# A mixture-of-experts layer: each expert's weights and row numbers are read together with the last quarter of its rows

## The chip, the core and the metric

The kernel runs on one core of a Trainium2 chip. The metric is the device time of one execution in microseconds. Three runs of the kernel before gave 1192.09, 1194.07 and 1198.56 us; the median is 1194.07 us. One further execution was taken by the hardware profiler: it took 1184.45 us, and all durations and instants below are from it, counted from the start of its span.

The core has five engines with an instruction stream each: TensorE (PE; its weight loads are PEld), VectorE (DVE), ScalarE (ACT), GpSimd (POOL) and SyncE (SP). SP only issues transfers here, and GpSimd issues transfers with row numbers taken from a tile (indirect DMA). All transfers run on 16 DMA engines.

## The reference

The input `x` is 16 x 128 x 512 in float32. Two blocks follow each other, each with a residual:

```
x = x + xattn(layernorm(x), ctx)          # 8 heads over 128 channels, rotary positions
x = x + ffn(layernorm(x))                 # a mixture of 32 experts, over 2048 rows of 512

def ffn(rows):                            # the second block, cut to what matters
    logits = rows @ gate_w.T              # 2048 x 32
    sel_w, sel_e = top_k(logits, 8)
    w = softmax(sel_w)                    # 8 weights for each row, scattered to 2048 x 32
    g, u = rows @ w_gate_proj[e].T, rows @ w_up_proj[e].T      # 192 wide, each expert e
    return sum over e of (silu(g) * u * w[:, e]) @ w_down_proj[e].T
```

The kernel computes only the chosen pairs of row and expert.

## The kernel before

**The attention stage** (to about 620 us) normalizes, attends and projects 16 blocks of 128 rows. For each row it also computes the 8 experts, the weights and a slot in each chosen expert's list. An expert's list has `CAP` = 576 slots in `xslot`, a DRAM tensor of 32 x 576 rows of `ROW` = 560 floats. A row there is 512 normalized values, then the row's 32 weights (from column `WCOL` = 512), then its row number in the output (column `NCOL` = 544), then padding; 2240 bytes in all. GpSimd writes such rows to their slots by indirect DMA (`put`, L519 to L530).

**The expert stage** goes through 32 places `i`. The first `GIVEN` = 4 places are fixed experts (31 to 28), of which slots 0 to 255 (`EARLY`) are computed inside the attention stage (`early_read`, `early_turn`, `early_up`, `early_down`, `early_add`), with small tiles of their own. The other 28 experts are sorted by their number of rows, and place `i` computes `SIZES[i]` slots: 576 down to 516 at places 4 to 21, 512 to 492 at places 22 to 31. Which expert stands at a place is known only when the kernel runs, so from place 4 on its weights are picked by a mask, `whose` (L800). Each expert passes through these steps:

- `fetch(i)` (L1008), on SP: `read_rows` (L816) reads the slots' rows into `xg`, four transfers, one for each quarter of 128 columns. Quarter `a` goes to partitions 32a to 32a+31; slot 32b + j lands on partition 32a + j, at block b. `read_notes` (L839) then reads weights and row number of each slot, the notes, into a tile of another shape: slot 128m + p on partition p, column m. It takes one transfer for the first 512 slots (L847), one for the rest if there is any (L849), and at odd places a third for the row numbers of the rest (L851). Then come the expert's own matrices, `wgu` (L113) and `wd` (L114).
- `prepare(i)` (L1027), on VectorE: `turn_rows` (L828) transposes 32 x 32 blocks, so that `xt` holds the rows' columns on partitions (L833). `use_notes` (L854) makes the row numbers whole numbers (`to`, L859 and L861) and multiplies the 32 weights by the mask and sums them (L869, L875), so that `weight` has one number for each slot. At the four given places the expert is known and the weight is taken straight from the notes tile.
- `up` (L878): three chains of four products on TensorE for each half of the slots (L892), into PSUM tiles of `ps_u` (four of them); silu on ScalarE (L901, L904), and the product with the other half's result on VectorE (L902, L910).
- `down` (L918): products with `wd` (L927, L931), then the multiplication by `weight`, one tile of 128 slots on ScalarE (L972), the next on VectorE (L970). `settle_rest` (L977) does the slots past 512 of two places at once: the odd place's rest lies on partitions 64 on, so that its weights must lie there too (`REST` = 64), while its row numbers lie from partition 0.
- `add` (L943), on GpSimd: one indirect DMA for each tile of 128 slots adds it to the output's rows (L946). The adds of one expert may run beside each other; those of the next wait until they have landed, since a row has several experts.

**What sets the order.** Instructions stand on each engine's stream as the code issues them (`manual_schedule`). At place `i` the code issues `fetch(i + 2)`, then the first half of `up(i)`, then `prepare(i + 1)` (on VectorE it thus stands between the two halves of `up`), the second half, and `down` of place `i - 1`. `xg` has two buffers: the rows for place `i + 2` are read once those of place `i` have been used. `to`, `notes` and `weight` have four: `use_notes(i)` waits until the adds of place `i - 4` have read `to`. `yb`, the weighted outputs, has three.

Of the kernel before, what the change touches and what calls it, by code (L numbers as in the profile page):

```python
# [10 lines left out]
F32 = mybir.dt.float32  # L11
I32 = mybir.dt.int32
AF = mybir.ActivationFunctionType
ALU = mybir.AluOpType
AX = mybir.AxisListType
PSUM = bass.MemoryType.PSUM

P = 128
B, C, T = 16, 128, 512
# [4 lines left out]
E, I, TOPK = 32, 192, 8  # L24
# [4 lines left out]
CAP = 576  # L29
HALF = CAP // 2  # L30
NB = CAP // 32
FULL, REST = divmod(CAP, P)
NM = FULL + 1
# [3 lines left out]
GIVEN = 4  # L37
# [6 lines left out]
EARLY, CUT = 256, 13  # L44
# [4 lines left out]
WCOL, NCOL = T, T + E  # L49
# [10 lines left out]
def kernel(  # L60
# [16 lines left out]
    nc = tc.nc  # L77
# [32 lines left out]
    def load_expert(e, name):  # L110

        wgu_sb, wd_sb = new_weights(name)
        nc.sync.dma_start(wgu_sb, wgu[e])  # L113
        nc.sync.dma_start(wd_sb, wd[e])  # L114
        return wgu_sb, wd_sb
# [5 lines left out]
    with ExitStack() as actx:  # L121
# [528 lines left out]
        ready = []  # L650
# [162 lines left out]
        nc.vector.tensor_reduce(most, beyond, AX.XY, ALU.max)  # L813
        nc.vector.tensor_copy(over, most)

    def read_rows(rows, n, name, pieces=1, begin=0):  # L816

        xg = xp.tile([P, CAP // 32, P], F32, tag="xg", name=f"xg{name}")
        step = (n - begin) // 32 // pieces
        for b0 in range(begin // 32, n // 32, step):  # L820
            for a in range(4):
                nc.sync.dma_start(
                    xg[32 * a : 32 * (a + 1), b0 : b0 + step, :],
                    rows[32 * b0 : 32 * (b0 + step), a * P : (a + 1) * P].rearrange("(b j) q -> j b q", j=32),
                )
        return xg

    def turn_rows(xg, n, name, pieces=1, begin=0):  # L828

        xt = xp.tile([P, NK, CAP], F32, tag="xt", name=f"xt{name}")  # L830
        step = (n - begin) // 32 // pieces
        for b0 in range(begin // 32, n // 32, step):
            nc.vector.transpose(  # L833
                xt[:, :, 32 * b0 : 32 * (b0 + step)].rearrange("p c (b j) -> p b c j", j=32),
                xg[:, b0 : b0 + step, :].rearrange("p b (c i) -> p b c i", i=32),
            )
        return xt

    def read_notes(i, rows, n):  # L839

        notes = xp.tile([P, NM, E + 1], F32, tag="notes", name=f"notes_{i}", bufs=4)
        more = max(n - FULL * P, 0)
        half = slice(i % 2 * REST, i % 2 * REST + more)
        full = rows[0 : FULL * P, WCOL : NCOL + 1].rearrange("(m p) w -> p m w", p=P)
        nc.sync.dma_start(notes[:, 0:FULL, :], full)  # L847
        if more:
            nc.sync.dma_start(notes[half, FULL, :], rows[FULL * P : n, WCOL : NCOL + 1])  # L849
            if i % 2:  # L850
                nc.sync.dma_start(notes[0:more, FULL, E : E + 1], rows[FULL * P : n, NCOL : NCOL + 1])  # L851
        return notes

    def use_notes(i, notes, n):  # L854

        to = xp.tile([P, NM], I32, tag="to", name=f"to_{i}", bufs=4)
        more = max(n - FULL * P, 0)
        half = slice(i % 2 * REST, i % 2 * REST + more)
        nc.vector.tensor_copy(to[:, 0:FULL], notes[:, 0:FULL, E])  # L859
        if more:  # L860
            nc.vector.tensor_copy(to[0:more, FULL : FULL + 1], notes[0:more, FULL, E : E + 1])  # L861
        if i < GIVEN:
            return notes[:, :, E - 1 - i], to

        own = xp.tile([P, NM, E], F32, tag="own", name=f"own_{i}")
        weight = xp.tile([P, NM], F32, tag="weight", name=f"weight_{i}", bufs=4)
        for part, m0, m1 in ((slice(0, P), 0, FULL), (half, FULL, NM))[: 1 + (more > 0)]:
            k = part.stop - part.start
            nc.vector.tensor_tensor(  # L869
                own[part, m0:m1, :],  # L870
                notes[part, m0:m1, 0:E],
                whose[part, i - GIVEN, :].unsqueeze(1).to_broadcast([k, m1 - m0, E]),
                ALU.mult,
            )
            nc.vector.tensor_reduce(weight[part, m0:m1], own[part, m0:m1, :], AX.X, ALU.add)  # L875
        return weight, to

    def up(w, xt, n, name, parts=None, h=None, between=None):  # L878
# [129 lines left out]
    def fetch(i):  # L1008


        if i < GIVEN:
            e = E - 1 - i
        else:
            e = nc.values_load(
                numbers[0:1, i - GIVEN : i - GIVEN + 1],
                engines=[mybir.EngineType.SP],
                min_val=0,
                max_val=E - 1,
                skip_runtime_bounds_check_because="the lowest five bits",
            )  # L1020
        n = SIZES[i]
        rows = xslot[e * CAP : (e + 1) * CAP, :] if i < GIVEN else xslot[bass.ds(e * CAP, CAP), :]
        xg = read_rows(rows[:, 0:T], -(-n // 32) * 32, f"_{i}", 1 if i else 2, EARLY * (i < GIVEN))
        notes = read_notes(i, rows, n)
        return ready[i] if i < GIVEN else load_expert(e, i), xg, notes

    def prepare(i, w, xg, notes):  # L1027
        n = SIZES[i]
        xt = turn_rows(xg, -(-n // 32) * 32, f"_{i}", 1 if i else 2, EARLY * (i < GIVEN))
        return w, xt, use_notes(i, notes, n)  # L1030


    with tc.manual_schedule(engines=set(mybir.ALL_ENGINES) - {mybir.EngineType.Pool}):
# [210 lines left out]
```

## Time and profile before

| what | value |
|---|---|
| median of three runs | 1194.07 us |
| profiled execution, its own time | 1184.45 us |
| its span, first to last instruction | 1182.7 us |
| mean granted TensorE clock | 0.987 |
| transfers of SP (q1): packets, MB, share of 16 engines | 137640, 135.17, 43.4% |
| transfers of GpSimd (q0): packets, MB, share of 16 engines | 32608, 76.85, 27.9% |
| packets under 512 bytes, of all | 38308 of 177829 |
| VectorE: turned rows, L833 | 33 in 74.2 us |
| VectorE: row numbers, L859 | 32, median 129 ns |

The page of a profile gives busy time and number of instructions of each engine, the groups of instructions that cost most (line, engine, operation, output<-inputs, shapes, number; then busy time and mean, then the idle time of the engine ahead of them and what ended it) and the queues of transfers. In a timeline a line has the start, the length, engine, code line, operation, tiles and number, and in brackets the idle time before it and what ended that. Such a releaser is inferred: where an instruction waits for several things, the name is that of the one that came last by the profile. A share of the DMA engines over 1 is possible, as packets of several queues overlap.

### The profile page before, as it was taken

How to read it: one execution, taken by the hardware profiler on the slowest of the kernel's cores; microseconds unless marked ns; L12 is line 12 of the kernel's file. 1: busy time of each engine (PE TensorE's matmuls, PEld its weight loads, DVE VectorE, ACT ScalarE, POOL GpSimd, SP SyncE). 2: the span in 40 equal slices, each digit the busy share in tenths (PEclk: the TensorE clock that was granted, in tenths of full speed). 3: DMA queues.
4: the chain of work that ended last, by engine and by line, in shares of the span. 5: the costliest groups of instructions: out<-in, count | busy, mean ns of one | idle time of the engine just before them, and what ended most of it. 6: DMA issues, size and time to landing. Idle time of an engine off the chain costs nothing. (4 is left out here: it accounts for less than half of the span.)

```text
span 1182.7 us, 17253 instructions
## 1 busy us (share of the span) xinstructions
PE 1136.4 (96%) x5868; PEld 568.8 (48%) x5868; DVE 703.6 (59%) x1432; ACT 442.9 (37%) x833; POOL 609.0 (51%) x629
## 2 busy tenths in 40 slices
PE   7999999999999999999989999999999999999990
PEld 3333333333333333333365566676666667777670
DVE  5777878888888887887554453444444344433430
ACT  1266656566556655556541111112112121211120
POOL 3324443467877888665446333453443445434444
PEclk9999999999999999999999999999999999999995
DMA  5878888857566767453459899999999999999955
GB/s 181 289 279 309 315 306 315 312 200 240 184 201 215 245 229 259 147 186 145 139 173 251 158 246 233 205 230 207 211 208 189 212 207 228 229 232 215 172 75 70
DMA packets 177829, 255.51 MB, mean 216 GB/s; under 512 B 38308, under 2 KB 108580, under 8 KB 177736
## 3 DMA queue, kind: packets, MB, share of 16 engines
q1 hardware_dynamic: 137640, 135.17, 43.4%
q0 software_dynamic: 32608, 76.85, 27.9%
q10 hardware_dynamic: 7488, 42.34, 9.2%
q8 instruction: 48, 0.79, 0.3%
q14 instruction: 45, 0.37, 0.1%
HBM read 114.63 MB, written 131.01 MB: 208 GB/s over the span
## 5 line engine op out<-in xcount | busy, mean ns | idle before, releaser
L345 DVE TENSOR_REDUCE maxes_sb<-s 128x1 f32<-128x512 f32 x512 | 329.3, 685 | 97.1 <-PE s L340 78.9
L946 POOL DMA_INDIRECT out_dram<-yb,to x142 | 219.5, 1546 | 287.9 <-DMA out_dram<-yb,to 110.9
L347 ACT ACTIVATE p<-s 128x512 f32<-128x512 f32 x512 | 278.2, 594 | 217.6 <-PE s L340 209.1
L892 PE MATMUL psu<-xt,wgu 128*128 128x252 f32 (+19 forms) x1416 | 328.4, 392 | 3.9 <-DVE xt L833 2.6
L332 PE MATMUL s<-k,q 32*128 32x512 f32 x1024 | 313.8, 640 | 1.4 <-DVE maxes_sb L345 1.1
L892 PEld LDWEIGHTS psu<-xt,wgu 128*128 128x128 f32 x1416 | 267.4, 191 | 76.5 <-ACT yb L972 14.3
L340 PE MATMUL s<-qa,k 32*128 32x512 f32 x1024 | 292.9, 641 | 2.1 <-ACT p L347 2.1
L332 PEld LDWEIGHTS s<-k,q 32*128 32x128 f32 x1024 | 93.9, 183 | 155.9 <-DVE maxes_sb L345 121.8
L521 POOL DMA_INDIRECT xslot<-row,slot x128 | 130.2, 1017 | 36.4 <-issue 33.5
L369 PE MATMUL av<-p,vt_sb 128*32 128x512 f32 x1024 | 137.0, 608 | 0.0
L927 PE MATMUL psy<-wd,h 128*128 128x512 f32 x240 | 108.5, 592 | 0.0
L281 POOL TENSOR_TENSOR straight<-straight,rope_sb 128x512 f32<-128x512 f32 x31 | 39.4, 1272 | 124.0 <-DMA other<-straight 108.3
L970 DVE TENSOR_SCALAR yb<-psy,weight 128x512 f32<-128x512 f32 (+5 forms) x56 | 42.1, 751 | 90.3 <-PE psy L931 87.4
L904 ACT ACTIVATE s<-psu 64x252 f32<-64x252 f32 (+19 forms) x59 | 22.8, 386 | 191.9 <-PE psu L892 178.5
L910 DVE TENSOR_TENSOR h<-psu,s 64x128 f32<-64x128 f32 (+16 forms) x166 | 43.0, 259 | 75.8 <-ACT s L904 74.1
L340 PEld LDWEIGHTS s<-qa,k 32*128 32x128 f32 x1024 | 78.6, 183 | 10.7 <-ACT p L347 10.5
L972 ACT ACTIVATE yb<-psy,weight 128x512 f32<-128x512 f32 x56 | 38.5, 687 | 118.8 <-PE psy L931 114.7
L902 DVE TENSOR_TENSOR h<-psu,s 128x252 f32<-128x252 f32 (+19 forms) x59 | 25.7, 436 | 88.2 <-PE psu L892 87.0
L833 DVE STREAM_TRANSPOSE xt<-xg 128x2176 f32<-128x2176 f32 (+4 forms) x33 | 74.2, 2251 | 1.1
L369 PEld LDWEIGHTS av<-p,vt_sb 128*32 128x32 f32 x1024 | 20.4, 108 | 97.2 <-issue 78.8
L927 PEld LDWEIGHTS psy<-wd,h 128*128 128x128 f32 x240 | 45.3, 189 | 44.8 <-issue 41.2
L931 PE MATMUL psy<-wd,h 64*128 64x512 f32 x240 | 60.4, 618 | 0.0
(139 smaller groups left out, 915.6 us busy)
## 6 DMA issues: line engine op xcount, KB each, us to landing
xslot<-empty_sb ACTq DMA_DIRECT2D x48, 840.0 KB
wgu<-in_wgu_dram SPq DMA_DIRECT2D x28, 768.0 KB
wd<-in_wd_dram SPq DMA_DIRECT2D x28, 512.0 KB
xg<-xslot SPq DMA_DIRECT2D x48, 272.0 KB
xg<-xslot SPq DMA_DIRECT2D x40, 256.0 KB
other<-straight SPq DMA_DIRECT2D x64, 128.0 KB
spread<-straight SPq DMA_DIRECT2D x64, 128.0 KB
k<-spread SPq DMA_DIRECT2D x32, 256.0 KB
```

The costliest lines, as they stand in the source:

```text
L332: nc.tensor.matmul(p1, q[rows, tt * P : (tt + 1) * P], k[rows, :], start=True, stop=True)
L340: nc.tensor.matmul(p2, k[rows, sc * P : (sc + 1) * P], qa[rows, :], start=True, stop=True)
L345: nc.vector.tensor_reduce(to, p1, AX.X, ALU.max)
L347: nc.scalar.activation(pr, p2, AF.Exp, scale=HD**-0.5)
L369: nc.tensor.matmul(av[j * SLOT : (j + 1) * SLOT, :], vt[:, at : at + SLOT], pairs.pop((u, sc, j)), start=(sc == 0), stop=(sc == NT - 1),)
L521: op = nc.gpsimd.indirect_dma_start(out=xslot[0 : (E - k) * CAP, :], out_offset=bass.IndirectOffsetOnAxis(ap=st["slot", b][:, k : k + 1], ...
L833: nc.vector.transpose(xt[:, :, 32 * b0 : 32 * (b0 + step)].rearrange("p c (b j) -> p b c j", j=32), xg[:, b0 : b0 + step, :].rearrange("p ...
L892: nc.tensor.matmul(p[:, 0:half], wgu_sb[:, kk, ch * P : (ch + 1) * P], xt[:, kk, cols], start=(kk == 0), stop=(kk == NK - 1),)
L910: nc.vector.tensor_tensor(h2[to : to + IR, lo:hi], ps[2][IR:P, at], s2[IR:P, at], ALU.mult)
L927: nc.tensor.matmul(y, h1[:, rows], wd_sb[:, 0, :], start=True, stop=False)
L931: nc.tensor.matmul(y, h2[to : to + IR, rows], wd_sb[to : to + IR, 1, :], start=False, stop=True,)
L946: op = nc.gpsimd.indirect_dma_start(out=out, out_offset=bass.IndirectOffsetOnAxis(ap=to[0:k, m : m + 1], axis=0), in_=yb[0:k, m, :], in_of ...
```

## The change

The notes are no longer read by themselves. The tile `xg` gets 33 more columns in each block (161 floats, 644 bytes, where there were 128 floats, 512 bytes), and the transfer of the last quarter reads 161 columns instead of 128, so that weights and row numbers land behind the last 128 values, on partitions 96 to 127: slot 32b + j on partition 96 + j, at block b. The transposes read 128 of the 161 columns.

`use_notes` now works from there. From place 4 on it multiplies by the mask and sums on these 32 partitions, for all blocks at once (512 to 576 elements for each partition). Then it copies row numbers and weights into the old layout: block b belongs to partitions 32(b mod 4) on of column b // 4, so for each of the four groups of 32 partitions one copy to `to` and one to `weight` takes all full columns, and each block past slot 512 takes two more, its weights 64 partitions higher at odd places. The given places copy their weights too, for the blocks from slot 256 on. In the instruction streams VectorE has 376 instructions in `use_notes` where it had 146, and SP 65 transfers fewer. The early part of the four given experts keeps its notes as they were.

```diff
@@ -813,15 +813,17 @@
         nc.vector.tensor_reduce(most, beyond, AX.XY, ALU.max)
         nc.vector.tensor_copy(over, most)
 
-    def read_rows(rows, n, name, pieces=1, begin=0):
-
-        xg = xp.tile([P, CAP // 32, P], F32, tag="xg", name=f"xg{name}")
+    def read_rows(rows, n, name, pieces=1, begin=0, more=0):
+
+
+        xg = xp.tile([P, CAP // 32, P + E + 1], F32, tag="xg", name=f"xg{name}")
         step = (n - begin) // 32 // pieces
         for b0 in range(begin // 32, n // 32, step):
             for a in range(4):
+                k = P + more * (a == 3)
                 nc.sync.dma_start(
-                    xg[32 * a : 32 * (a + 1), b0 : b0 + step, :],
-                    rows[32 * b0 : 32 * (b0 + step), a * P : (a + 1) * P].rearrange("(b j) q -> j b q", j=32),
+                    xg[32 * a : 32 * (a + 1), b0 : b0 + step, 0:k],
+                    rows[32 * b0 : 32 * (b0 + step), a * P : a * P + k].rearrange("(b j) q -> j b q", j=32),
                 )
         return xg
 
@@ -832,47 +834,41 @@
         for b0 in range(begin // 32, n // 32, step):
             nc.vector.transpose(
                 xt[:, :, 32 * b0 : 32 * (b0 + step)].rearrange("p c (b j) -> p b c j", j=32),
-                xg[:, b0 : b0 + step, :].rearrange("p b (c i) -> p b c i", i=32),
+                xg[:, b0 : b0 + step, 0:P].rearrange("p b (c i) -> p b c i", i=32),
             )
         return xt
 
-    def read_notes(i, rows, n):
-
-
-
-        notes = xp.tile([P, NM, E + 1], F32, tag="notes", name=f"notes_{i}", bufs=4)
-        more = max(n - FULL * P, 0)
-        half = slice(i % 2 * REST, i % 2 * REST + more)
-        full = rows[0 : FULL * P, WCOL : NCOL + 1].rearrange("(m p) w -> p m w", p=P)
-        nc.sync.dma_start(notes[:, 0:FULL, :], full)
-        if more:
-            nc.sync.dma_start(notes[half, FULL, :], rows[FULL * P : n, WCOL : NCOL + 1])
-            if i % 2:
-                nc.sync.dma_start(notes[0:more, FULL, E : E + 1], rows[FULL * P : n, NCOL : NCOL + 1])
-        return notes
-
-    def use_notes(i, notes, n):
-
-        to = xp.tile([P, NM], I32, tag="to", name=f"to_{i}", bufs=4)
-        more = max(n - FULL * P, 0)
-        half = slice(i % 2 * REST, i % 2 * REST + more)
-        nc.vector.tensor_copy(to[:, 0:FULL], notes[:, 0:FULL, E])
-        if more:
-            nc.vector.tensor_copy(to[0:more, FULL : FULL + 1], notes[0:more, FULL, E : E + 1])
+    def use_notes(i, xg, n):
+
+
+
+        first, last = (EARLY if i < GIVEN else 0) // 32, -(-n // 32)
         if i < GIVEN:
-            return notes[:, :, E - 1 - i], to
-
-        own = xp.tile([P, NM, E], F32, tag="own", name=f"own_{i}")
-        weight = xp.tile([P, NM], F32, tag="weight", name=f"weight_{i}", bufs=4)
-        for part, m0, m1 in ((slice(0, P), 0, FULL), (half, FULL, NM))[: 1 + (more > 0)]:
-            k = part.stop - part.start
+            weights = xg[3 * 32 : P, :, P + E - 1 - i]
+        else:
+
+            own = xp.tile([P, CAP // 32, E], F32, tag="own", name=f"own_{i}", bufs=1)[3 * 32 : P, 0:last, :]
             nc.vector.tensor_tensor(
-                own[part, m0:m1, :],
-                notes[part, m0:m1, 0:E],
-                whose[part, i - GIVEN, :].unsqueeze(1).to_broadcast([k, m1 - m0, E]),
+                own,
+                xg[3 * 32 : P, 0:last, P : P + E],
+                whose[3 * 32 : P, i - GIVEN, :].unsqueeze(1).to_broadcast([32, last, E]),
                 ALU.mult,
             )
-            nc.vector.tensor_reduce(weight[part, m0:m1], own[part, m0:m1, :], AX.X, ALU.add)
+            weights = xp.tile([P, CAP // 32], F32, tag="sum", name=f"sum_{i}", bufs=1)[3 * 32 : P, :]
+            nc.vector.tensor_reduce(weights[:, 0:last], own, AX.X, ALU.add)
+        to = xp.tile([P, NM], I32, tag="to", name=f"to_{i}", bufs=4)
+        weight = xp.tile([P, NM], F32, tag="weight", name=f"weight_{i}", bufs=4)
+        full = min(last, 4 * FULL)
+        for q in range(4):
+            rows, m0 = slice(32 * q, 32 * (q + 1)), first // 4
+            m1 = m0 + len(range(first + q, full, 4))
+            nc.vector.tensor_copy(to[rows, m0:m1], xg[3 * 32 : P, first + q : full : 4, P + E])
+            nc.vector.tensor_copy(weight[rows, m0:m1], weights[:, first + q : full : 4])
+        for b in range(full, last):
+            q = b % 4
+            nc.vector.tensor_copy(to[32 * q : 32 * (q + 1), FULL : FULL + 1], xg[3 * 32 : P, b : b + 1, P + E])
+            q += i % 2 * (REST // 32)
+            nc.vector.tensor_copy(weight[32 * q : 32 * (q + 1), FULL : FULL + 1], weights[:, b : b + 1])
         return weight, to
 
     def up(w, xt, n, name, parts=None, h=None, between=None):
@@ -1020,14 +1016,13 @@
             )
         n = SIZES[i]
         rows = xslot[e * CAP : (e + 1) * CAP, :] if i < GIVEN else xslot[bass.ds(e * CAP, CAP), :]
-        xg = read_rows(rows[:, 0:T], -(-n // 32) * 32, f"_{i}", 1 if i else 2, EARLY * (i < GIVEN))
-        notes = read_notes(i, rows, n)
-        return ready[i] if i < GIVEN else load_expert(e, i), xg, notes
-
-    def prepare(i, w, xg, notes):
+        xg = read_rows(rows, -(-n // 32) * 32, f"_{i}", 1 if i else 2, EARLY * (i < GIVEN), E + 1)
+        return ready[i] if i < GIVEN else load_expert(e, i), xg
+
+    def prepare(i, w, xg):
         n = SIZES[i]
         xt = turn_rows(xg, -(-n // 32) * 32, f"_{i}", 1 if i else 2, EARLY * (i < GIVEN))
-        return w, xt, use_notes(i, notes, n)
+        return w, xt, use_notes(i, xg, n)
 
 
     with tc.manual_schedule(engines=set(mybir.ALL_ENGINES) - {mybir.EngineType.Pool}):
```

## Prediction

> **What bounds the kernel now.** I read the page first: TensorE is busy nearly everywhere, VectorE is half idle in the expert stage, and GpSimd's costliest line there is the indirect add into the output.
>
> ```profile
> span 1182.7 us, 17253 instructions
> PE 1136.4 (96%) x5868; PEld 568.8 (48%) x5868; DVE 703.6 (59%) x1432; ACT 442.9 (37%) x833; POOL 609.0 (51%) x629
> L946 POOL DMA_INDIRECT out_dram<-yb,to x142 | 219.5, 1546 | 287.9 <-DMA out_dram<-yb,to 110.9
> ```
>
> Then the windows of 20 us through the expert stage (columns: length; busy us and count of PE, PEld, DVE, ACT, POOL; granted clock; DMA share; GB/s), and TensorE's waits.
>
> ```profile
> 1020.00:1040.00 20.00, 20.00 (x78) 12.68 (x76) 7.38 (x16) 3.44 (x7) 9.61 (x7) 1.00 1.12 254
> 1140.00:1160.00 20.00, 15.81 (x64) 10.88 (x64) 4.22 (x9) 3.50 (x7) 11.34 (x8) 0.96 0.60 79
> 1160.00:1180.00 20.00, 0.00 (x0) 0.00 (x0) 0.00 (x0) 0.00 (x0) 7.25 (x5) 0.50 0.56 77
> PE psu L892 <- DVE xt L833: 2.6, 2, 2.4
> ```
>
> From 680 to 1140 us every window has 20.00 of 20 us of TensorE at full clock. In the whole run it waits 2.6 us for turned rows (2.36 of it before the first product of L892) and never for an expert's rows, notes or weights as such. TensorE stops at 1155.8; then only GpSimd works. So two things set the end: TensorE's stream, which this change leaves as it is, and the chain of adds behind it. GpSimd's timeline shows that chain:
>
> ```profile
> 1063.62 1.57 POOL L946 DMA_INDIRECT out_dram<-yb,to  x1 [11.57 <-ACT s L901]
> 1084.29 1.57 POOL L946 DMA_INDIRECT out_dram<-yb,to  x1 [12.89 <-DMA out_dram<-yb,to]
> 1100.29 1.57 POOL L946 DMA_INDIRECT out_dram<-yb,to  x1 [8.80 <-DMA out_dram<-yb,to]
> ...
> 1165.87 1.56 POOL L946 DMA_INDIRECT out_dram<-yb,to  x1 [4.87 <-issue]
> 1171.49 1.55 POOL L946 DMA_INDIRECT out_dram<-yb,to  x1 [0.30 <-issue]
> ```
>
> Each line but the last is the first add of one expert (places 24, 25, 26, 31); it waits in brackets until the adds of the expert before have landed. Up to place 21 GpSimd waits once a pair for the shared last tile (L1003), so it is not behind. From place 22 to the end it waits for landings only: place 30's outputs are ready at 1140.7 and added from 1153.93. With every landing at the trace's shortest, 4.6 us, place 31 would end near 1160.3 (its last outputs are ready at 1156.6, two adds of 1.86 follow) and not at 1173.0. So 12.7 us hang on landings.
>
> **The change, part by part.**
>
> *Notes' transfers go.* 65 issues leave SP (32 of L847, 22 of L849, 11 of L851), at medians of 0.99, 1.00 and 0.33 us. SP waits in the same stretch for released buffers and landings, so this shortens no path by itself: the rows of the place after next are issued at 1033.25 and turned at 1062.44. In packets some 17,100 of 132 bytes go, 540 an expert. The trace's packet records between 690 and 1000 us give a mean of 22.9 ns for 132 bytes and 44.0 ns for 512: 540 x 22.9 / 16 engines = 0.77 us of every DMA engine per expert.
>
> *The last quarter's rows grow to 644 bytes.* 544 packets an expert by 132 bytes; a 6144-byte packet takes 245 ns (median), 25 bytes per ns, so 5.3 ns each: 544 x 5.3 / 16 = +0.18 us.
>
> *All four quarters now land at a step of 644 bytes, not 512.* No row of this trace shows 512 bytes written so. [...] Bounds 0 and +12 ns; I take +3, nearer the row. 2176 packets x 3 / 16 = +0.41 us per expert (0 to 1.63). Sum of the DMA parts: -0.77 + 0.18 + 0.41 = -0.2 us per expert (-0.6 to +1.0).
>
> *VectorE's new work.* Now, at a place without rest:
>
> ```profile
> 1030.91 2.31 DVE L833 STREAM_TRANSPOSE xt<-xg 128x2048 f32<-128x2048 f32 x1
> 1033.15 0.13 DVE L859 CAST to<-notes 128x4 int32<-128x4 f32 x1
> 1033.18 0.28 DVE L869 TENSOR_TENSOR own<-notes,whose 128x128 f32<-128x128 f32 x1
> 1033.50 0.29 DVE L875 TENSOR_REDUCE weight<-own 128x4 f32<-128x128 f32 x1
> 1033.82 0.42 DVE L902 TENSOR_TENSOR h<-psu,s 128x254 f32<-128x254 f32 x1
> 1035.42 0.78 DVE L910 TENSOR_TENSOR h<-psu,s 64x2 f32<-64x2 f32 x3 [1.18 <-ACT s L904]
> 1039.49 1.61 DVE L970 TENSOR_SCALAR yb<-psy,weight 128x512 f32<-128x512 f32 x2 [3.30 <-PE psy L931]
> ```
>
> Three instructions, 0.67 us to L902. After: the product on 32 partitions has 512 elements (L800 has 1024 in 1.38 us, L869 128 in 0.28: 0.75), the sum has 512 (L345 reduces 512 in 0.69), then 8 copies at 16 blocks of 32 slots (places 22 to 31), 10 at 17 and 12 at 18. The cast and the unrelated product behind it start 0.03 to 0.04 us apart, so they overlap: 8 such copies would take 0.13 + 7 x 0.04 = 0.4 us. [...] Sum 0.75 + 0.69 + 0.84 + gaps 0.1 = 2.4 us against 0.67: +1.7; at 18 blocks 3.1 (0.83 + 0.75 + 1.4 + 0.1) against 1.05 (681.17 to 682.25): +2.0. With about 1.3 us more at each of the four given places, some 55 us for the run: VectorE from 704 to about 760 us, 64%.
>
> What hides it: L902 and L910 start 1.7 us later, and L970 waits 3.30 us for TensorE anyway. The PSUM tile that L902 frees is next written by the third chain of the following `up`, near 1043.7, 9 us later. Without that cover it would cost 28 x 1.7 = 48 us. It is thinnest at place 5: VectorE waits at L859 until 694.57 for place 1's adds (4.81 us), and then TensorE wants that tile at 697.3, with 1.0 us to spare; of the new work product and sum come before that wait, and the copies behind it take about 1.5 us where 1.2 stand now: +0.3, hidden. In the start, VectorE idles 3.47 us before 645.87 and gets 2.6 us more; the first turned rows still come ahead of any copy, so L892 starts at 639.53.
>
> *The wait for `to` now also holds `xg`.* The wait itself exists (L859, 12.5 us in five). Behind it stand the copies and L902, as before; new is that SP's read of the place after next waits until the copies are done: 2.4 us later normally, 5 us at 1083.5. One notes issue (1 us with its gaps) is gone, so the weights start about 1.4 us later, and have over 20 us to spare (by the packet records those issued at 1040.33 have landed near 1049, and are for place 27, whose products start near 1071.6). Cost 0; which adds these transfers meet shifts, by up to 3 us either way.
>
> *Sum.* Nothing on TensorE's path. On the chain of adds -0.2 us at each of the six landings (places 22 to 27) that share the queues with reads: -1 us. The profiled execution took 1184.45 us (span 1182.7, 1.75 around it), so 1183.4; it lies 9.6 below the median of 1194.07, so the forecast is **1193**.
>
> **The rivals.**
>
> [...]
>
> 2. *Faster: the landings shorten.* Over 4.6 us, the waits behind places 22 to 26 hold 3.2 + 7.0 + 8.3 + 4.2 + 2.2 = 25 us. If a third goes with the notes' packets and SP's later reads, the end comes 8 us earlier: 1186; the floor is 1181. Against: place 28's adds landed only after 8.54 us with no reads about, so some of it is not SP's.
>
> 3. *VectorE decides.* If a copy costs the 0.46 us of the slowest cast at L859, 12 copies are 5.5 us, and places 4 to 6 stall TensorE by 1 to 2 us each: 1197. Against: the median cast takes 0.129.
>
> If 644-byte rows were split into 512 and 132, packets would not fall; about +0.6 us an expert, 1196, within the forecast's spread.
>
> **The numbers.** Forecast 0.45 and third rival 0.05 make 0.50 for within 0.5% (6 us, about what a measurement of this kernel tells from none); faster 0.22; slower 0.28. The forecast's own range is 1188 to 1200; to leave out no more than a tenth on each side it reaches to 1184 (most of the second rival) and 1208 (most of the first).
>
> **What would show it.** Right: L892 still starts near 639.5 and TensorE is full until about 1155; 512-byte packets under 50 ns; VectorE near 760 us; L970 still waiting for TensorE. Wrong: TensorE waits at L892 for VectorE or rows; packets over 56 ns; the last add moved by more than 6 us.

## The result and the profile after

The changed kernel is slower. Over 21 runs its median is 1199.24 us (1190.52 to 1216.09), and that of the kernel before, on the same chip, is 1191.94 us (21 runs, 1183.13 to 1208.34). The ratio of their times is **1.0079**, with a 95% interval of 1.0056 to 1.0101. All ratios here leave disturbed runs out. The profiled execution took 1199.19 us for a span of 1197.3, against 1184.45 and 1182.7 before. That pair lies 14.7 us apart, twice as far as the medians, because the profile of before was one of its fastest executions. From the first product of the expert stage to the end of the last add it is 545.1 us after and 533.5 before: 11.6 us. The rest of the 14.7 us comes mainly from the attention stage (that first product starts 2.85 us later), which the change touches in four early places only; its length differs by several microseconds between profiles that run the same code up to there (the first product starts at 639.53 us in the kernel before, at 649.46 in the same with eight tiles for `to`).

Here is the top of the page, then the costliest line of GpSimd from the groups of instructions, then the transfers:

```profile
span 1197.3 us, 17295 instructions
PE 1139.5 (95%) x5868; PEld 569.3 (48%) x5868; DVE 760.1 (63%) x1662; ACT 442.5 (37%) x833; POOL 609.9 (51%) x629
...
DMA packets 159421, 255.41 MB, mean 213 GB/s; under 512 B 19900, under 2 KB 90172, under 8 KB 159328
...
q1 hardware_dynamic: 119232, 135.07, 41.7%
...
L942 POOL DMA_INDIRECT out_dram<-yb,to x142 | 221.3, 1559 | 299.4 <-DMA out_dram<-yb,to 154.3
```

VectorE has 56.5 us more work, SP's queue has 18,408 packets and 1.7 points of the DMA engines less: what was meant to go has gone. But GpSimd now waits 154.3 us for landings of adds, where it waited 110.9. The windows (the same columns as before the change) show TensorE ending later:

```profile
1020.00:1040.00 20.00, 20.00 (x85) 14.93 (x85) 11.90 (x24) 3.65 (x8) 9.33 (x6) 1.00 1.11 272
1140.00:1160.00 20.00, 18.91 (x78) 13.02 (x76) 9.86 (x23) 3.21 (x7) 9.34 (x6) 1.00 0.44 57
1160.00:1180.00 20.00, 9.23 (x37) 5.79 (x36) 2.51 (x5) 2.13 (x4) 9.77 (x7) 0.85 0.73 99
```

TensorE had nothing after 1155.8; now 9.23 us of its work lie behind 1160. The waits of TensorE and VectorE (total us, times, longest) say for what it waited:

```profile
PE psy L923 <- DVE h L898: 4.6, 2, 3.5
PE psu L888 <- DVE h L898: 2.8, 2, 2.2
...
DVE to L865 <- DMA out_dram<-yb,to: 38.3, 6, 8.3
```

The first two did not exist before: TensorE waits for L898 (L902 before the change), VectorE's product of the halves. VectorE's wait at the first copy to `to`, for the adds of four places earlier, is 38.3 us where it was 12.5 (and one more of 3.04 us, at 1083.54, that the profile puts down to `issue`). Before the change its line was:

```profile
DVE to L859 <- DMA out_dram<-yb,to: 12.5, 5, 4.8
```

Laid against each other, the starts of L888 and L892 part in two places: by 4.8 us at places 4 and 5, and by 7.4 us at places 28 to 31. In between the distance stays at 6.04 us, for 24 places. So neither the transfers nor VectorE's longer work cost TensorE anything at most places. At places 4 and 5 VectorE's first copies to `to` are:

```profile
690.38 0.16 DVE L865 CAST to<-xg 32x4 int32<-32x4 f32 x1 [8.07 <-DMA out_dram<-yb,to]
...
702.13 0.16 DVE L865 CAST to<-xg 32x4 int32<-32x4 f32 x1 [4.15 <-DMA out_dram<-yb,to]
```

The late part is read from three timelines of the changed kernel (start, length, engine, line, operation, tiles, number, idle time before). First GpSimd's, the first adds of places 24 to 28 and 31:

```profile
1075.59 1.57 POOL L942 DMA_INDIRECT out_dram<-yb,to  x1 [14.00 <-DMA out_dram<-yb,to]
...
1095.63 1.57 POOL L942 DMA_INDIRECT out_dram<-yb,to  x1 [12.26 <-DMA out_dram<-yb,to]
...
1112.52 1.57 POOL L942 DMA_INDIRECT out_dram<-yb,to  x1 [9.69 <-DMA out_dram<-yb,to]
...
1129.33 1.58 POOL L942 DMA_INDIRECT out_dram<-yb,to  x1 [9.60 <-DMA out_dram<-yb,to]
...
1141.13 1.56 POOL L942 DMA_INDIRECT out_dram<-yb,to  x1 [4.59 <-DMA out_dram<-yb,to]
...
1180.33 1.56 POOL L942 DMA_INDIRECT out_dram<-yb,to  x1 [4.54 <-issue]
```

Ahead of places 24 to 27 it waits 45.6 us, before the change 40.1 (11.57, 12.89, 8.80, 6.82). Counted from the first product of the expert stage, place 22's first add starts 6.3 us later than before the change, place 28's 12.3 and place 31's 11.6. From place 22 on every first add waits for landings, before the change and after: its outputs are ready earlier (place 29's at about 1137, added from 1157.13). So these adds decide the end, and the 7.4 us that TensorE loses at places 28 to 31 do not: they only show how late the landings were.

Then VectorE at place 28, and SP's reads of the rows of places 29 to 31:

```profile
1094.88 0.16 DVE L865 CAST to<-xg 32x4 int32<-32x4 f32 x1 [6.90 <-DMA out_dram<-yb,to]
1094.96 0.15 DVE L866 COPY weight<-sum 32x4 f32<-32x4 f32 x1
1095.13 0.16 DVE L865 CAST to<-xg 32x4 int32<-32x4 f32 x1
...
1095.63 0.20 DVE L865 CAST to<-xg 32x4 int32<-32x4 f32 x1
...
1095.93 0.42 DVE L898 TENSOR_TENSOR h<-psu,s 128x252 f32<-128x252 f32 x1
```

```profile
1075.88 1.94 SPq L824 DMA_DIRECT2D xg<-xslot  x4
...
1095.86 1.96 SPq L824 DMA_DIRECT2D xg<-xslot  x4
...
1112.80 1.94 SPq L824 DMA_DIRECT2D xg<-xslot  x4
```

The adds of place 24 land near 1094.8. That starts two things: VectorE's copies of place 28, which need `to` free, and the adds of place 25 (1095.63). The last read of `xg` ends at 1095.83, and SP issues the rows of place 30 at 1095.86, on top of those adds. In all three lines SP starts 0.3 us behind the first add: **the two are locked together**. The packets of the trace, started in each 2 us of such a meeting, show what comes of it:

| after, us | 512- and 644-byte (rows) | 6144- and 4096-byte (weights) | 2048-byte (adds) |
|---|---|---|---|
| 1077 to 1079 | 840 | 0 | 0 |
| 1079 to 1081 | 317 | 0 | 126 |
| 1081 to 1083 | 732 | 1 | 13 |
| 1083 to 1085 | 143 | 35 | 115 |
| 1085 to 1089 | 0 | 198 | 138 |

The adds issued from 1075.59 on move almost nothing while rows flow in the first and third row. (Part of the first row is the usual delay: with no reads about, as at 1129.33 or 1141.13, the first packet of an add starts 2.1 us after its issue; here it took 3.4.) Late adds mean a later end of the wait at place 29, and so the next read again falls on the next adds. Before the change, SP issued rows at these times, while the adds started at 1063.62, 1084.29 and 1100.29:

```profile
1064.78 2.44 SPq L822 DMA_DIRECT2D xg<-xslot  x4
...
1080.53 2.26 SPq L822 DMA_DIRECT2D xg<-xslot  x4
...
1096.24 1.94 SPq L822 DMA_DIRECT2D xg<-xslot  x4
```

Its clock was then set by the turns on VectorE, 15.7 us apart, not by the adds (each issue follows the end of a turn, at 1064.75, 1080.50 and 1096.21, by 0.03 us): the first read fell 1.2 us behind them, the other two 3.8 and 4.1 us ahead.

### The profile page after: what moved, and what is told of

It reads as the page before. It is cut to its first block, busy times and chain, and to the rows that moved or that the text cites. A ratio compares the mean times of both kernels' runs of the same rounds, so it can differ in the third digit from the quotient of the medians.

```text
span 1197.3 us, 17295 instructions
## 1 busy us (share of the span) xinstructions
PE 1139.5 (95%) x5868; PEld 569.3 (48%) x5868; DVE 760.1 (63%) x1662; ACT 442.5 (37%) x833; POOL 609.9 (51%) x629
## 3 DMA queue, kind: packets, MB, share of 16 engines
q0 software_dynamic: 32608, 76.85, 28.2%
## 5 line engine op out<-in xcount | busy, mean ns | idle before, releaser
L942 POOL DMA_INDIRECT out_dram<-yb,to x142 | 221.3, 1559 | 299.4 <-DMA out_dram<-yb,to 154.3
L888 PE MATMUL psu<-xt,wgu 128*128 128x252 f32 (+19 forms) x1416 | 329.1, 392 | 7.2 <-DVE h L898 2.8
L888 PEld LDWEIGHTS psu<-xt,wgu 128*128 128x128 f32 x1416 | 267.3, 191 | 80.6 <-ACT yb L968 14.3
L968 ACT ACTIVATE yb<-psy,weight 128x512 f32<-128x512 f32 x60 | 41.2, 687 | 134.9 <-PE psy L927 134.9
L966 DVE TENSOR_SCALAR yb<-psy,weight 128x512 f32<-128x512 f32 (+5 forms) x60 | 44.7, 750 | 54.8 <-PE psy L927 51.8
L898 DVE TENSOR_TENSOR h<-psu,s 128x252 f32<-128x252 f32 (+19 forms) x59 | 25.7, 436 | 74.7 <-PE psu L888 73.8
```

Source lines behind the costliest of these rows:

```text
L888: nc.tensor.matmul(p[:, 0:half], wgu_sb[:, kk, ch * P : (ch + 1) * P], xt[:, kk, cols], start=(kk == 0), stop=(kk == NK - 1),)
L942: op = nc.gpsimd.indirect_dma_start(out=out, out_offset=bass.IndirectOffsetOnAxis(ap=to[0:k, m : m + 1], axis=0), in_=yb[0:k, m, :], in_of ...
L966: nc.vector.tensor_scalar_mul(yb[0:k, m, :], y, weight[0:k, m : m + 1])
```

## The experiments

All kernels ran 14 to 22 times, most of them 22, beside the kernel before on the same chip. The first theories were: T1, the wait for `to`, behind which `xg` is now held and L898 queued; T2, VectorE's longer work by itself; T3 (T3' in some expectations), that SP is no longer held at place 4. (Before the change, L847 at place 4 waited 9.6 us for the notes tile of place 0, up to 669.67, with that place's weights behind it; after, they were issued from 662.64 on.)

**Without the wait.** The changed kernel with more tiles, so that nothing waits for the adds of four places before; and the same on the kernel before, as a control:

```diff
-        to = xp.tile([P, NM], I32, tag="to", name=f"to_{i}", bufs=4)
+        to = xp.tile([P, NM], I32, tag="to", name=f"to_{i}", bufs=8)
```

> The changed kernel with eight buffers of `to` in place of four, so that VectorE does not wait for the adds of four places before. T1 (the wait for `to` now stands in front of the release of `xg`, so SP's reads start together with the next adds, these land late, and the loop holds up VectorE and TensorE): the waits of 38.3 us at the copies to `to` are gone, TensorE's waits for L898 (7.4 us) are gone, ratio to before 0.998 to 1.003. T2 (VectorE's 55 us of added work decide): ratio stays at 1.008. T3 (without the notes SP has more transfers in flight, and they keep the adds back whatever VectorE does): landings stay about 1 us longer and the chain of adds ends late, ratio 1.004 or more.

> The kernel before with eight buffers of `to`: the control for e1. All theories: VectorE's 12.5 us of waits at `to` go, but TensorE waited for none of them, so 0.997 to 1.001. If it is faster than that, the wait for `to` cost the kernel before too, and e1 must be read against this run.

Measured: 1.0023 (0.9996 to 1.0049), and 1.0012 (0.9988 to 1.0037) for the control. VectorE no longer waits for adds, and of TensorE's waits for L898 this is left:

```profile
PE psy L923 <- DVE h L898: 0.8, 1, 0.8
```

Most of the loss is taken through this wait. VectorE has as much to do as in the changed kernel (763.7 us), so that work alone is not the loss: T1 is borne out so far, T2 is not.

**One part alone, put into the kernel before.** In the first, a small copy of `xg` behind the casts holds `xg` as the changed kernel does; in the second, VectorE gets a product, a sum and 8 to 12 copies into tiles that nothing reads (ahead of and behind the casts as in the changed kernel); in the third, SP isn't held at place 4:

```diff
+        held = xp.tile([P, 1], F32, tag="held", name=f"held_{i}", bufs=1)
+        nc.vector.tensor_copy(held, xg[:, EARLY // 32, 0:1])
```

```diff
+            nc.vector.tensor_tensor(more_own, whose[3 * 32 : P, 0:last, :], whose[3 * 32 : P, 1 : last + 1, :], ALU.mult)
+            nc.vector.tensor_reduce(sums[:, 0:last], more_own, AX.X, ALU.add)
...
+                nc.vector.tensor_copy(spare[32 * q : 32 * (q + 1), k, m0:m1], sums[:, first + q : full : 4])
```

```diff
-        notes = xp.tile([P, NM, E + 1], F32, tag="notes", name=f"notes_{i}", bufs=4)
+        notes = xp.tile([P, NM, E + 1], F32, tag="notes", name=f"notes_{i}", bufs=8)
```

> The kernel before, with one copy of 128 numbers out of `xg` on VectorE behind the casts to `to`, so that `xg` is released only after that wait; notes and everything else as before. T1: slower, 1.003 to 1.008, with waits at `to` over 25 us (12.5 before) and landings of 10 us and more in the last places. T2 and T3: 1.000 within 0.2%, waits at `to` as before.

> The kernel before with the changed kernel's new VectorE work added on spare tiles: a product and a sum of 480 to 576 numbers on 32 partitions and the 8 to 12 small copies at each place, its own notes work kept, and no hold on `xg`. T2 (the amount of work decides): 1.004 to 1.008, TensorE waiting for L898's product. T1 and T3': 0.999 to 1.002, VectorE's idle time at L970 and L902 taken up, TensorE as before.

> The kernel before with eight buffers of the notes tile in place of four. In the kernel before, SP waits at the notes of place 4 for the last use of place 0's notes (9.6 us at L847), which holds back 1.28 MB of weights and the rows behind them while the adds of places 0 and 1 are on their way; the change took this hold away with the transfers. T3' (that hold protected the adds): without it the waits ahead of the adds of places 0 to 2 grow from 4.5, 6.5 and 8.3 us to 8 to 11, the waits at `to` of places 4 and 5 from 6.4 us together to 10 or more, TensorE loses 2 to 5 us there, ratio 1.002 to 1.005. T1 alone, T2: no difference, 1.000 (as far as 1.001).

Measured: held `xg` 1.0030 (1.0009 to 1.0051), with 16.7 us of the wait for `to` at L859 and no wait of TensorE for L902's result; VectorE's work 1.0016 (0.9991 to 1.0042); eight notes tiles 1.0012 (0.9985 to 1.0040). None of them is the whole loss, and only the first is clear of no change. With the work alone the wait is even short:

```profile
DVE to L868 <- DMA out_dram<-yb,to: 3.0, 3, 1.5
```

**Parts together.** Held `xg` and the work; and all three:

> The kernel before with two parts of the change at once: the 128x1 copy of xg behind the wait for `to`, and the spare product, sum and eight to twelve copies of VectorE. Alone they gave 1.0030 and 1.0016. If the two only add (theory A), the ratio is 1.0035 to 1.0055 and TensorE waits for h under 3 us. If they enforce each other, as in the changed kernel (theory B: the wait for `to` pushes work that is longer by 1.8 us a place, and the reads start later for it), 1.006 to 1.010, with over 25 us of waits at the casts and over 4 us of TensorE waits for h.

> The same as the run before it, and eight tiles for the notes, so that SP is no longer held at place 4: all three parts of the change that the runs so far point to, still with the notes' transfers. Theory C (these three are the whole loss, and the transfers that the change removes bring nothing): 1.0065 to 1.0095, the changed kernel's value. If the lost hold of SP at place 4 adds nothing to the other two: within 0.001 of the run before it. If something else in the change costs (the row step, the copies' partition groups): under 1.005.

Measured: 1.0006 (0.9972 to 1.0040) and 1.0028 (1.0004 to 1.0051), the second with 6.6 us of waits at the casts. This was the miss that mattered: the three parts I had named do not make the loss, and those waits are not there. With the work added, the 1.0030 of the hold is no longer clear of no change.

**The early hold, and an early release.** In the changed kernel, SP is held at place 4 by a 4-byte transfer out of place 0's last `yb` tile, with that place's weights behind it (the gate), alone and with eight tiles for `to`. In two others the notes are copied out of `xg` ahead of the wait, so that `xg` comes free before it, with four and with eight tiles for `to`:

```diff
...
+                gate = sort.tile([P, 1], F32, tag="gate", name="gate")
+                nc.sync.dma_start(gate[0:1, :], outs[0][0][0:1, FULL, 0:1])
+                fetched[GIVEN] = load_expert(later.pop(), GIVEN), fetched[GIVEN][1]
```

```diff
+        own_notes = xp.tile([P, CAP // 32, E + 1], F32, tag="stage", name=f"stage_{i}", bufs=1)[3 * 32 : P]
+        nc.vector.tensor_copy(own_notes[:, first:last, :], xg[3 * 32 : P, first:last, P : P + E + 1])
```

> The changed kernel with SP held again at place 4: the weights of place 4 are issued behind a 4-byte transfer that waits for place 0's last tile of outputs, as its notes did in the kernel before. T3': the waits ahead of the first adds return to about 4.5 and 6.5 us and TensorE's loss at places 4 and 5 (4.8 us) goes; the lock-step at the end can remain, ratio 1.002 to 1.006. T1 alone or T2: 1.007 to 1.008.

> The changed kernel with both: eight buffers of `to`, and SP held at place 4. T1 with T3': nothing of the loss is left, 0.998 to 1.001, and the adds of the first places are as in the kernel before. T2 or another cause: 1.002 and more, as with eight buffers alone.

> The changed kernel, with the notes copied out of `xg` to a tile of their own (one VectorE copy of 512 to 594 numbers on 32 partitions, about 0.4 us) ahead of the wait for `to`; `to` keeps four buffers. The release of `xg` no longer stands behind the wait, the wait itself stays, and VectorE works 12 us more. T1: most of the loss goes, 0.999 to 1.004, waits at `to` back under 20 us. T2: 1.008 to 1.010. T3: 1.004 or more.

> The changed kernel with eight tiles for `to` and with the notes copied out of xg first. Eight tiles alone gave 1.0023, the copy alone 1.0047. If the wait for `to` is the only thing that made the early release of xg worth anything, 1.0015 to 1.0040 (the copy is 0.3 us of VectorE a place for nothing). If xg's release at the end of the copies still delays SP's reads, 0.998 to 1.001.

Measured, in this order: 1.0030 (0.9998 to 1.0062), 1.0009 (0.9980 to 1.0039), 1.0047 (1.0024 to 1.0069), 1.0005 (0.9978 to 1.0033). With the gate alone the late lock remains (waits of 13.22, 12.71, 9.40 and 9.15 us ahead of places 24 to 27). Without a wait for `to` the loss is gone in both; with it, an earlier release of `xg` leaves 1.0047, whose interval meets that of the changed kernel: 20.7 us of waits at `to` are left, and TensorE still waits 4.0 us for VectorE's product. Yet the late lock is gone there, with 6.66 and 7.11 us ahead of places 26 and 27 and SP reading 5.0 us and more ahead of the adds of places 25 and 26. What is left stands before it: place 22's first add is 7.0 us late, counted from the first product as above, and place 31's 6.8. With the gate it is the reverse: 3.4 us at place 22, 8.9 at place 31. So the lock is one of two parts of the loss, the delay up to place 22 the other.

**The transfers themselves.** One thing of the change was in none of these kernels except the changed ones: the notes' transfers are gone. So they were put back into the changed kernel, into tiles that nothing reads (`read_notes` as before the change, with eight tiles); and they were taken out of the kernel before, where places 4 to 31 then use the notes of places 0 to 3, alone and with held `xg` and VectorE's work. (These two add their rows at the wrong places, and SP's hold at place 4 goes with the transfers.) The changed kernel itself ran again beside them:

```diff
+        read_notes(i, rows, n)
         return ready[i] if i < GIVEN else load_expert(e, i), xg
```

```diff
     def read_notes(i, rows, n):
+        if i >= GIVEN:
+            return kept[i % GIVEN]
...
+        kept[i] = notes
```

> The changed kernel itself, once more, on the same chip as the three runs below: 1.006 to 1.010 if its loss is a property of the kernel; its waits at the copies to `to` over 30 us, and the adds of places 26 and 27 with 14.0 and 12.3 us ahead of their successors as in the first profile. Under 1.005 would say that the loss differs between sessions, and that single parts of 0.001 to 0.003 can't be told apart here.

> The changed kernel with the notes' old transfers put back into tiles that nothing reads: two or three more issues of SP a place between the rows and the weights. Theory D (the removed transfers let SP run ahead, so that its row reads lock to the start of the adds): the waits at `to` fall under 12 us and the ratio to 1.003 or less, the value of the kernel before with hold, work and eight notes tiles (1.0028). If the loss comes from what VectorE does with the columns or from the 644-byte step: 1.006 to 1.010 unchanged, or a little more, since the transfers cost 0.77 us of the DMA engines a place.

> The kernel before without the notes' transfers of places 4 to 31: these places use the notes of places 0 to 3, so weights and row numbers are those of other experts and the output isn't the reference's; the number of rows that the adds move may differ a little. Theory D alone (fewer transfers are enough for the loss): 1.005 to 1.009. If it needs the longer hold of xg and VectorE's work too: 0.997 to 1.003. If transfers are what they were priced at, 0.77 us of the DMA engines a place saved and nothing else: 0.996 to 1.000.

> The run before it with the 128x1 copy of xg behind the wait for `to` and the spare VectorE work: all of the change but the layout (the 644-byte step, the columns from one quarter of the partitions); weights and row numbers as in the run before it. Theory D with hold and work (the three together make the loss): 1.006 to 1.010, with over 25 us of waits at the casts. If the layout makes it: under 1.004.

Measured (the 14.0 and 12.3 us that the first expectation puts behind places 26 and 27 are those ahead of places 24 and 25):

| kernel | ratio (95%) | waits for `to`, us | ahead of places 24 to 27, us |
|---|---|---|---|
| changed, again | 1.0064 (1.0037 to 1.0091) | 37.5 | 14.01, 12.73, 9.80, 9.47 |
| changed, transfers put back | 0.9961 (0.9937 to 0.9985) | 10.2 | 9.78, 11.90, 7.27, 7.41 |
| before, transfers out | 1.0021 (0.9997 to 1.0044) | 30.5 | 14.26, 11.73, 6.45, 6.52 |
| before, transfers out, hold and work | 1.0065 (1.0043 to 1.0087) | 27.7 | 14.43, 11.45, 9.19, 8.74 |

The second row has all of the new layout and none of the loss; the fourth has none of the layout and a ratio like the changed kernel's. The third is not clear of no change. GpSimd's queue has 32,608 packets and 76.85 MB in the kernel before and in the third, so the adds' traffic is the same. Between the third and the fourth row the trace shows what the hold does. GpSimd without it:

```profile
1071.35 1.57 POOL L951 DMA_INDIRECT out_dram<-yb,to  x1 [14.26 <-DMA out_dram<-yb,to]
...
1090.86 1.57 POOL L951 DMA_INDIRECT out_dram<-yb,to  x1 [11.73 <-DMA out_dram<-yb,to]
...
1104.51 1.57 POOL L951 DMA_INDIRECT out_dram<-yb,to  x1 [6.45 <-DMA out_dram<-yb,to]
```

SP in the same kernel:

```profile
1069.29 1.94 SPq L822 DMA_DIRECT2D xg<-xslot  x4
...
1085.04 2.40 SPq L822 DMA_DIRECT2D xg<-xslot  x4
...
1100.75 1.94 SPq L822 DMA_DIRECT2D xg<-xslot  x4
```

And SP and GpSimd with hold and work:

```profile
1083.41 1.95 SPq L822 DMA_DIRECT2D xg<-xslot  x4
...
1102.55 1.95 SPq L822 DMA_DIRECT2D xg<-xslot  x4
...
1119.04 1.95 SPq L822 DMA_DIRECT2D xg<-xslot  x4
```

```profile
1083.82 1.57 POOL L973 DMA_INDIRECT out_dram<-yb,to  x1 [14.43 <-DMA out_dram<-yb,to]
...
1103.04 1.57 POOL L973 DMA_INDIRECT out_dram<-yb,to  x1 [11.45 <-ACT yb L999]
...
1119.44 1.57 POOL L973 DMA_INDIRECT out_dram<-yb,to  x1 [9.19 <-ACT yb L999]
```

Without the transfers both have one wait of over 14 us, at place 24. Where `xg` is free after the turns, SP reads 2.1, 5.8 and 3.8 us ahead of the adds, and the waits fall to 6.5 us. Where `xg` is held, each read starts within 0.5 us of the adds, three times in a row, and the waits stay at 9 us: the lock of the changed kernel, made from the kernel before. Hold and work were added together here; the hold without the work was not run without the transfers, so whether the work is needed stays open.

**Bytes or issues?** Last, the changed kernel with 4-byte transfers, as many as the notes had; the one with the transfers back, with eight tiles for `to`; and that one again as it was:

```diff
+        spacer = xp.tile([P, 4], F32, tag="spacer", name=f"spacer_{i}", bufs=8)
+        for k in range(1 + (n > FULL * P) * (1 + i % 2)):
+            nc.sync.dma_start(spacer[0:1, k : k + 1], rows[0:1, NCOL : NCOL + 1])
```

> The changed kernel with one to three 4-byte transfers a place in the places of the notes' old ones: as many issues of SP, and next to no bytes. In the kernel as built an issue waits for the landing of the one eight issues before, so this restores the spacing of SP without the 0.77 us of the DMA engines. If the number of issues is what counts (theory D in that form): 0.994 to 0.999, waits at `to` under 15 us. If the notes' transfers act by the time that they fill on the queue between rows and weights: 1.004 to 1.010, as the changed kernel.

> The changed kernel with the unread transfers and eight tiles for `to`: xg comes free at the end of the copies, without a wait in between. If the 10.2 us of waits at `to` that were left with the transfers still cost something: 0.992 to 0.996. If they are hidden: 0.995 to 0.998, as without the eight tiles. If the wait at `to` is what spaces SP in that kernel: 0.998 to 1.003.

> The changed kernel with the notes' old transfers put back unread, once more: 0.993 to 0.999 if its gain of 0.4% is a property of the kernel; 0.999 to 1.003 if it was luck of the first session.

Measured: 1.0004 (0.9977 to 1.0031), 0.9971 (0.9939 to 1.0002), 1.0000 (0.9963 to 1.0036). With the 4-byte transfers the lock is gone (GpSimd, then VectorE's wait in total):

```profile
1077.14 1.57 POOL L942 DMA_INDIRECT out_dram<-yb,to  x1 [9.65 <-DMA out_dram<-yb,to]
...
1095.28 1.57 POOL L942 DMA_INDIRECT out_dram<-yb,to  x1 [10.37 <-DMA out_dram<-yb,to]
...
1110.28 1.57 POOL L942 DMA_INDIRECT out_dram<-yb,to  x1 [7.38 <-ACT s L900]
```

```profile
DVE to L865 <- DMA out_dram<-yb,to: 10.6, 2, 5.6
```

SP reads rows at 1068.16, 1084.30 and 1099.38, about 9 to 11 us ahead of those adds. So it is SP's issues, not their bytes, whose absence opens the way to the lock. It is the lock that they take away, not the early delay: TensorE still waits 3.0 us for VectorE's product at place 5, and place 22's first add is 6.2 us late. But with 9.65, 10.37, 7.38 and 7.52 us ahead of places 24 to 27, place 28's is only 0.9 us late. By what means an issue more or less moves SP was argued, not shown. (In the traces SP's issues take eight semaphores, 100 to 107, in turn, and each waits on the one that it takes, so also for the landing of the issue eight before it: before the change, the issue at 1081.10 us waits on 104, which the one at 1064.78 took.) The gain of 0.4% with the transfers put back did not come again: no version is shown to beat the kernel before.

## Why the prediction was wrong

The forecast was no change, 1193 us; the ratio lies above the 0.5% that it allowed, while 1199.24 us lies within its range of 1184 to 1208. Its steps in turn:

- *The notes' transfers go*: the packets went as counted (17,124 of 132 bytes). **"So this shortens no path by itself"** asked only whether a path gets shorter, and not whether one gets longer. With the issues went what kept SP's reads apart from the adds: put back, bytes or no bytes, the loss is gone (1.0004 and 0.9961, then 1.0000); taken out of the kernel before, a wait of over 14 us appears at place 24, though by itself it costs nothing clear (1.0021, 0.9997 to 1.0044). I had seen that SP waits for buffers, but had not asked what fewer issues do to those waits.
- *644-byte rows* were costed at +5.3 ns: from 700 to 1010 us they take 56.4 ns on average against 41.2 for 512 bytes, +15 ns; over 544 packets that is 0.5 us a place of each of 16 engines, not 0.18. It did not reach the path.
- *The 644-byte step* stands in the sum at +3 ns (0 to +12); no run shows that term or its upper bound. What the runs show in its place: from 700 to 1010 us a 512-byte packet takes 41.2 ns on average, where it took 43.7 before, with the notes' 17,124 packets on the queue; and with the notes' transfers put back, so with as many packets as before, the kernel with the new step gave ratios of 0.9961 and 1.0000. No penalty shows; the lower bound was right.
- *VectorE's new work* was right: 760.1 us where about 760 was said. The sum of 2.4 us has 0.84 for eight copies, that of 3.1 has 1.4 for twelve: terms that no run shows. In their place, at place 28, the copies take 1.05 us from the first cast (1094.88) to L898 (1095.93), for four pairs: pairs start 0.25 us apart, and the second copy of a pair 0.08 us behind the first. So 0.84 and gaps came nearer than the 0.4 us of copies that start 0.04 us apart. The cover failed where the wait for `to` had grown, at places 4 and 5 and at 28 to 31: *"+0.3, hidden"* at place 5 assumed that place 4's wait stays at 1.62 us. It was 8.07, and with place 5's 4.15 the two passed 4.8 us to TensorE.
- *The wait for `to` now also holds `xg`*: **"Cost 0; which adds these transfers meet shifts, by up to 3 us either way"** is the step that failed. I took the wait's length from the trace of before as given and asked only whether the reads have time. They have; no product ever waited for rows or weights because of them. But where the wait ends at the landing of an add, a read released behind it starts with the next adds, and that is no shift to either side. It happened three times running (0.3 us behind the adds each time), and GpSimd's waits for the last two landings that followed were 9.69 and 9.60 us where reads 3.8 and 4.1 us ahead had left 8.80 and 6.82; so the next wait ended late again. What the runs show in place of a cost of 0: the hold alone 1.0030 (1.0009 to 1.0051), with VectorE's work 1.0006, and with the work and without the notes' issues 1.0065 (1.0043 to 1.0087); with no wait for `to` in the changed kernel 1.0023 (0.9996 to 1.0049).
- *The sum*, six landings shorter by 0.2 us each: of the four ahead of places 24 to 27, three became longer instead (14.00, 9.69 and 9.60 us where 11.57, 8.80 and 6.82 stood) and one shorter (12.26 for 12.89).

Of the rivals, rows that land more slowly at the new step, which the 1208 allows for, did not come (41.2 ns a packet of 512 bytes), and the landings did not shorten. (The trace of before has one wait of 4.48 us for a landing, shorter than the 4.6 that the prediction takes as the shortest; nothing hangs on it.) The third, that VectorE decides, named a sign that came true, TensorE waiting for VectorE, with a wrong cause: a copy does not cost 0.46 us (0.15 to 0.20 at place 28), and the same work in the kernel before gave 1.0016. That the number still fell into the wide range is luck: its sum held no term for any of this.

What stays open is how the 0.79% splits. In the profile 6.3 of the 11.6 us stand already at place 22's first add (TensorE's wait at places 4 and 5 among them) and the rest comes behind it; in the second profile of the changed kernel it is 3.8 of 11.1, and TensorE waits for no product at places 4 and 5 there. The ratios can't tell the two apart: the gate at place 4 gave 1.0030, but its interval, 0.9998 to 1.0062, meets that of the changed kernel.

## What to carry to other kernels

When a buffer's last use moves behind a wait for a transfer, its refill can start at that transfer's landing, together with whatever else was waiting for it (here 0.3 us behind the adds, three times running); draw both on one timeline before costing the hold at nothing. A transfer that looks like pure overhead may be what keeps two streams on the same DMA engines out of step (here 1.0064 without the notes' transfers, 1.0004 with 4-byte ones in their places), so a count of bytes saved says little where the end hangs on landings. If three parts of a change, put into the old kernel, do not add up to its loss, look for the part that was only taken away. And before a stall is counted as loss, see whether the chain that ends last waits for it: here 7.4 us of TensorE's waits at the end did not.

## What was not expected of the hardware

- In the changed kernel the packets of GpSimd's adds nearly stopped in stretches of SP's reads of rows: 732 row packets and 13 of the adds in the 2 us from 1081, with adds issued from 1075.59 on; 739 and 4 in the 2 us from 1101, 702 and 14 in those from 1118. With no reads about, the 2 us from 1135 hold 130 of the adds'. Behind the last issue of the group from 1075.59 GpSimd waits 12.26 us for its landing, where it waits 4.59 us behind place 27's, with no reads about.
- Rows of 512 bytes that land at a step of 644 bytes took no longer here than at one of 512: 41.2 against 43.7 ns on average from 700 to 1010 us, with the notes' packets gone.
- Two executions of one kernel can differ by more than the change: the profile of before was 7.5 us below its median, and the changed kernel with its transfers put back gave a ratio of 0.9961 one time and 1.0000 another.
